# Layer 3 of a four-layer graph kernel: two blocks of sources per step, count rows on four row groups, clamps on two engines

## The chip, the cores and the metric

The kernel runs on one core of a Trainium2 chip. The metric is the device time of one execution in microseconds, from first to last instruction of the core with what lies around it; lower is better. The engines are PE (TensorE: matmuls, with its weight loads listed as PEld), DVE (VectorE), ACT (ScalarE), POOL (GpSimd) and SP (SyncE, which here issues DMAs).

## The reference, cut to what matters

Four graph layers run one after the other on x (4096 x 64) and a 0/1 adjacency adj (4096 x 4096), each on `h = relu(layernorm(x))` and added to x. The change lies in layer 3:

```python
def _L3_gnn_ref(input, adj, weight, bias):          # MAX_NEIGH = 100, DECAY = 0.5
    support = input @ weight
    mask = (adj != 0).astype(support.dtype)
    rank = jnp.cumsum(mask, axis=1)
    deg = rank[:, -1:]
    k = jnp.minimum(deg, float(MAX_NEIGH))
    pos = rank - (deg - k)
    w = mask * jnp.where(pos > 0, DECAY ** (k - pos), 0.0)
    out = w @ support + bias
    return out
```

The last neighbour of a node has weight 1, the one before it 1/2, and so on, so `k - pos` is the number of neighbours that come after this one. Layer 2 just before it needs `adj @ h` and the degrees, then a 128 x 64 product, a relu and a row norm.

The kernel also checks, in every execution, that adj holds only 0 and 1. If it doesn't, a general kernel runs instead; with the given inputs it never does.

## The kernel before, in words

Nodes are in 32 blocks of 128 (`NB = 32`, `P = 128`). adj is given transposed, so sources lie on partitions and targets on the free axis. The mask as one byte per entry lies in DRAM as `mask_d`, in eight groups (`NQ = 8`) of four blocks (`JT = 4`).

The last function, `layers_fast`, holds layers 2 and 3. Layer 2 works in two halves of targets (`hf`). For each half it sums `h` over neighbours, and counts edges per source block and target (`dc`, `cnt16`, 32 rows of counts for each group of 512 targets, four groups on the 128 partitions). Four calls of `layer2_group` follow, each for 512 nodes: a long chain of small steps on PE, DVE and ACT that ends in `SS`, the fp16 high and low parts of `h @ weight`. The last step on DVE of each call is appended to `valued`. Then `plate` multiplies the counts by a triangle, which gives for each source block the number of edges in later blocks, and `late` is that, limited to 128, for half `hf`.

Layer 3 makes four passes `u`, each over 1024 targets (`HO2`, two groups of 512, `NK = 2`). In a pass it goes through the 32 source blocks `j`. For a block it makes the exponent in PSUM, in a tile `pv` of 128 x 1024 fp32 (two banks): first two matmuls with K = 32, which spread the row of `late` for this block to all 128 sources (L2751; the 32 rows are those of the target group, at partitions `r` to `r + 31`); then two matmuls of the triangular matrix `tri` with the mask bytes (L2759), which subtract the edges that follow inside the block. ACT clamps the result at 0 and writes it as int16 (L2768); those bits, read as bf16, are the power of two. Two matmuls with the `SS` of the block add them up in PSUM (`sacc`, L2733), one step late: the sums of block `j - 1` are written behind the exponent of block `j`. After 32 blocks the sums go through `ev`, a small product with `fold_3` and two additions to `out`.

The checks of adj use one half row block each: `count_odd` asks for 128 x 2048 fp32 (1 MB) into `raw` (two buffers, L954) and compares it on DVE (L955). There are 64 checks; 48 are done in layer 1, and 16 are written into layer 3, one at every block with `j % 8 == 4`. `tc.issue_after(valued[-1].ins)` keeps the DVE part of them behind the last step of layer 2 there.

The order on each engine is not the order of the text. The kernel's framework has a planner which goes through all instructions before the run, with estimates of duration, and gives each engine the earliest in the text among those whose inputs and buffers are ready; that order is then fixed, and each engine waits on semaphores in it. The number of buffers of a tile (`bufs`) therefore limits how far a load or a step runs ahead. Only some stretches before layer 3 have an order set by hand (`in_order`). PSUM in layer 3 has eight banks: two of `misc`, two of `sacc`, four of `pv`.

Of the kernel before, what the change touches and what calls it, by code (L numbers as in the profile page):

```python
# [9 lines left out]
F32 = mybir.dt.float32  # L10
BF16 = mybir.dt.bfloat16
F16 = mybir.dt.float16
F8 = mybir.dt.float8e4
I32 = mybir.dt.int32
I8 = mybir.dt.int8
I16 = mybir.dt.int16
U8 = mybir.dt.uint8
AF = mybir.ActivationFunctionType
ALU = mybir.AluOpType
AX = mybir.AxisListType  # L20
PSUM = bass.MemoryType.PSUM
# [3 lines left out]
P = 128  # L25
N = 4096
NB = N // P
D = 64
G = 512
NG = N // G  # L30
GB = G // P
JT = 4
# [803 lines left out]
def kernel(  # L836
# [24 lines left out]
    nc = tc.nc  # L861
    NH, F, O = W_sp.shape[0] + W_int.shape[0], W_sp.shape[1], W_sp.shape[2]
# [85 lines left out]

        return col.unsqueeze(2).to_broadcast([P, col.shape[1], width])

    def count_odd(pool, c):

        raw = pool.tile([P, HW], F32, name="raw", tag="raw", bufs=2)
        nc.sync.dma_start(raw, adjT[c % NB * P : (c % NB + 1) * P, c // NB * HW : (c // NB + 1) * HW])  # L954
        nc.vector.scalar_tensor_tensor(  # L955
            raw, raw, 0.0, raw, ALU.is_gt, ALU.not_equal, accum_out=bad[:, c : c + 1]
        )

    todo = iter(range(2 * NB))
# [81 lines left out]
    with ExitStack() as l0:  # L1041
        lp = l0.enter_context(tc.tile_pool(name="l0", bufs=1))
# [258 lines left out]
        with ExitStack() as pa:  # L1301
            hp = pa.enter_context(tc.tile_pool(name="prep", bufs=1))
            work = pa.enter_context(tc.tile_pool(name="pwork", bufs=2))
# [47 lines left out]
            with in_order():  # L1351
                nc.vector.tensor_reduce(fsum, FT[0:F, :], AX.X, ALU.add)
                for b0 in range(0, NB, 8):
                    pw = (ps, ps2)[b0 // 8 % 2].tile([P, 8, KZ], F32, name="pst", tag="misc")
                    for b in range(8):
# [3 lines left out]
                            rhs=rhz,  # L1359
# [1158 lines left out]
    def layers_fast(es, wide, *sums):  # L2518
# [75 lines left out]
        with not_before_nodes():  # L2594
# [25 lines left out]
            nc.vector.tensor_scalar(w3, w3, Q3[0:D], VAL, ALU.mult, ALU.mult)  # L2620
            fold_3 = lp.tile([P, D], F32, name="fold_3f")
            nc.vector.tensor_scalar(fold_3, fold_h, M3, 2.0**27 / VAL, ALU.mult, ALU.mult)
        late = lp.tile([P, 2, G], BF16, name="late")

        def layer2_group(b0, part, deg):

# [47 lines left out]
        with tc.tile_pool(name="ps_nacc", bufs=6, space=PSUM) as ps_acc:  # L2674
            for hf in range(2):
                accs = [ps_acc.tile([P, G], F32, name="nacc", tag="nacc") for _ in range(NS)]
                dc = ps_acc.tile([P, G], F32, name="dc", tag="nacc")
                for q in range(NQ):
                    m = work.tile([P, JT, HW], U8, name="m2", tag="m2", bufs=3)
                    nc.sync.dma_start(m, mask_d[q][hf])  # L2680
                    m8 = m.bitcast(F8)
                    for t in range(JT):
                        j = q * JT + t
                        for k in range(NS):
                            nc.tensor.matmul(  # L2685
                                accs[k],
                                lhsT=HH[:, j].rearrange("p s d -> p (s d)"),
                                rhs=m8[:, t, k * G : (k + 1) * G],
                                start=(j == 0),
                                stop=(j == NB - 1),  # L2690
                            )
                    for t in range(JT):
                        j = q * JT + t
                        for k in range(NS):
                            nc.tensor.matmul(
                                dc[k * O : (k + 1) * O, :],
                                lhsT=sel[:, j * O : (j + 1) * O],
                                rhs=m8[:, t, k * G : (k + 1) * G],
                                start=(j == 0),
                                stop=(j == NB - 1),  # L2700
                            )
                cf = work.tile([P, G], F32, name="cf", tag="cf")
                nc.vector.tensor_copy(cf, dc)
                nc.gpsimd.tensor_copy(cnt16[:, hf], cf)
                ev = work.tile([P, NS, G], F32, name="ev2", tag="ev2", bufs=1)
                for k in range(NS):
                    (nc.vector.tensor_copy if k % 2 else nc.scalar.copy)(ev[:, k, :], accs[k])
                pd = ps.tile([P, GB, NS], F32, name="pdeg", tag="misc")
                for b in range(GB):
                    nc.tensor.matmul(  # L2710
                        pd[:, b], lhsT=cf[:, b * P : (b + 1) * P], rhs=qsel, start=True, stop=True
                    )
                deg = work.tile([P, NS, GB], F32, name="degf", tag="degf")
                nc.vector.tensor_scalar(
                    deg.rearrange("p q b -> p b q"), pd, 1.0, 1.0, ALU.add, ALU.max
                )
                nc.vector.reciprocal(deg, deg)
                for g in range(NS):
                    layer2_group(hf * HB + g * GB, ev[:, g, :], deg[:, g, :])
                pl = ps.tile([P, G], F32, name="plate", tag="misc")  # L2720
                nc.tensor.matmul(pl, lhsT=lat, rhs=cnt16[:, hf], start=True, stop=True)
                nc.vector.tensor_scalar(late[:, hf], pl, VBITS, None, ALU.min)


        ps_acc = es.enter_context(tc.tile_pool(name="ps_sacc", bufs=2, space=PSUM))
        ps_v = es.enter_context(tc.tile_pool(name="ps_v", bufs=2, space=PSUM))
        for u in range(4):
            hs = slice((u % 2) * HO2, (u % 2 + 1) * HO2)
            accs = [ps_acc.tile([P, G], F32, name="sacc", tag="sacc") for _ in range(NK)]

            def add_up(j, w):
                for k in range(NK):
                    nc.tensor.matmul(  # L2733
                        accs[k],
                        lhsT=SS[:, j].rearrange("p s d -> p (s d)"),
                        rhs=w[:, k * G : (k + 1) * G].bitcast(BF16),
                        start=(j == 0),
                        stop=(j == NB - 1),
                    )

            last = None
            for q in range(NQ):
                m = work.tile([P, JT, HO2], U8, name="m3", tag="m3", bufs=3)
                nc.sync.dma_start(m, mask_d[q][u // 2][:, :, hs])
                for t in range(JT):
                    j = q * JT + t

                    pv = ps_v.tile([P, HO2], F32, name="pv", tag="pv")
                    for k in range(NK):
                        r = ((u % 2) * NK + k) * O  # L2750
                        nc.tensor.matmul(  # L2751
                            pv[:, k * G : (k + 1) * G],
                            lhsT=blk[r : r + O, j, :],
                            rhs=late[r : r + O, u // 2, :],
                            start=True,
                            stop=False,
                        )
                    for k in range(NK):
                        nc.tensor.matmul(  # L2759
                            pv[:, k * G : (k + 1) * G],  # L2760
                            lhsT=tri,
                            rhs=m[:, t, k * G : (k + 1) * G].bitcast(F8),
                            start=False,
                            stop=True,
                        )

                    w = work.tile([P, HO2], I16, name="w3b", tag="w3b", bufs=3)
                    nc.scalar.activation(w, pv, AF.Relu)  # L2768
                    if j % 8 == 4:
                        with tc.issue_after(valued[-1].ins):  # L2770
                            count_odd(work, next(todo))
                    if last is not None:
                        add_up(*last)
                    last = (j, w)
            add_up(*last)
            ev = work.tile([P, NK, G], F32, name="ev3", tag="ev3")
            for k in range(NK):
                (nc.vector.tensor_copy if k % 2 else nc.scalar.copy)(ev[:, k, :], accs[k])
            for k in range(NK):
                b0 = (u * NK + k) * GB  # L2780
                pn = ps.tile([P, GB, D], F32, name="pn3", tag="misc")
                for b in range(GB):
                    nc.tensor.matmul(
                        pn[:, b, :],
                        lhsT=ev[:, k, b * P : (b + 1) * P],
                        rhs=fold_3,
                        start=True,
                        stop=True,
                    )
                og = work.tile([P, GB, D], F32, name="og", tag="og")  # L2790
                nc.vector.tensor_tensor(og, pn, b3t.unsqueeze(1).to_broadcast([P, GB, D]), ALU.add)
                nc.vector.tensor_tensor(og, og, x[:, b0 : b0 + GB, :], ALU.add)
                nc.gpsimd.dma_start(  # L2793
                    out[b0 * P : (b0 + GB) * P, :].rearrange("(b p) f -> p b f", p=P), og
                )
# [92 lines left out]
```

## Time and profile before

The kernel took 2023.15 us, the median of three runs (2019.92, 2023.15, 2024.01).

| | |
|---|---|
| time of the profiled execution | 2021.7 us |
| its span, first to last instruction | 2019.9 us |
| mean granted TensorE clock | 0.941 |
| busy: PE, DVE, ACT | 90%, 76%, 73% of the span |
| layer 3, first and last count matmul | 1808.9 to about 2007 us |
| `ev` of passes u = 0 to 3 on DVE | 1877.7, 1921.8, 1965.6, 2009.8 us |
| DMA in the whole span | 239.05 MB, mean 118 GB/s |

Busy times count the time in which an engine works on at least one instruction. A row of the costliest groups names the source line, the engine, the operation, output and inputs, shapes and count, then busy microseconds and the mean nanoseconds of one, and after the bar the idle time just before these instructions and what ended it. Matmuls overlap in PE's pipeline: a duration of some 385 ns is from entry to exit, while the next may start after 215 ns.

### The profile page before, as it was taken

Reading aid. Unit: us, or ns where it says so; the run is one execution under the profiler, and the core shown is the slowest. Engines: PE = TensorE matmul, PEld = TensorE weight load, DVE = VectorE, ACT = ScalarE, POOL = GpSimd, SP = SyncE. Lnnn points to the kernel's source line nnn. Section 1 sums busy time; section 2 is a strip of 40 time slices with the busy share of each in tenths; the row PEclk is TensorE's granted clock in tenths of the full one; section 3 lists DMA queues with packets and bytes.
Section 4 is the critical chain, followed back from the end, with each engine's and each line's share of the span. In section 5 each row is a group of like instructions: output and inputs, shape, how many; then the busy total and the mean of one; then the engine's idle time right before and its main releaser. Section 6 shows DMA issues by size and latency. Waiting matters only on the chain. (4 is left out here: it accounts for less than half of the span.)

```text
span 2019.9 us, 44190 instructions
## 1 busy us (share of the span) xinstructions
PE 1810.5 (90%) x19340; PEld 818.8 (41%) x19340; DVE 1534.4 (76%) x2239; ACT 1474.5 (73%) x1439; POOL 83.4 (4%) x125
## 2 busy tenths in 40 slices
PE   5889989999999999996699958999999985899998
PEld 3444445444444444444244432333333333454332
DVE  6779988998789879996778768888878788533530
ACT  3768888899789888993789857777777743227676
POOL 2000100100000000001011100000000000000000
PEclk8999999999999999997799968999999997889999
DMA  8945564424311111103355415444344336312752
GB/s 112 183 113 100 101 101 65 154 117 172 111 49 49 49 49 54 54 2 96 111 177 194 157 48 199 142 146 153 123 142 150 114 121 221 125 63 73 280 199 65
DMA packets 117016, 239.05 MB, mean 118 GB/s; under 512 B 11062, under 2 KB 84006, under 8 KB 102054
## 3 DMA queue, kind: packets, MB, share of 16 engines
q1 hardware_dynamic: 101996, 192.95, 28.4%
q0 software_dynamic: 14816, 43.18, 11.9%
q8 instruction: 153, 2.51, 0.5%
q14 instruction: 51, 0.42, 0.1%
HBM read 245.37 MB, written 49.46 MB: 146 GB/s over the span
## 5 line engine op out<-in xcount | busy, mean ns | idle before, releaser
L1205 ACT ACTIVATE st<-srow,nt 128x2048 int8<-128x2048 f32 x352 | 682.8, 1994 | 78.4 <-DVE B L1211 77.5
L1211 DVE TENSOR_TENSOR B<-st,mres 128x1024 int32<-128x1024 int32 x256 | 311.7, 1220 | 68.0 <-PE accC L1541 43.5
L1541 PE MATMUL accB<-B,ybh 128*32 128x512 fp8e4 x3072 | 338.7, 384 | 15.6 <-DVE B L1211 15.6
L1541 PE MATMUL accD<-B,ybh 128*32 128x512 fp8e4 x2048 | 301.3, 387 | 21.9 <-DVE h L1657 21.9
L1541 PEld LDWEIGHTS <-ybh 128*32 128x32 bf16 (+1 forms) x6656 | 197.0, 98 | 237.7 <-issue 75.9
L1541 PE MATMUL accC<-B,ycn 128*32 128x512 fp8e4 x2272 | 267.8, 381 | 1.2 <-issue 1.2
L1541 PE MATMUL accC<-mres,ych 128*32 128x512 fp8e4 x2272 | 267.7, 381 | 0.0
L1541 PE MATMUL accL<-B,ybh 128*32 128x512 fp8e4 x1536 | 220.4, 390 | 4.6 <-DVE h L1661 4.5
L1541 PEld LDWEIGHTS <-ych 128*32 128x32 f16 x4096 | 168.7, 98 | 114.5 <-issue 9.1
L1199 DVE TENSOR_SCALAR st<-srow,nt 128x2048 uint8<-128x2048 f32 x160 | 205.4, 1284 | 2.5
L2336 PE MATMUL accj<-sg,who 128*64 128x512 f32 (+1 forms) x512 | 196.6, 614 | 6.5 <-DVE sg L2329 6.1
L2336 PE MATMUL acci<-sg,who 128*64 128x512 f32 (+1 forms) x512 | 196.7, 614 | 0.0
L955 DVE SCALAR_TENSOR_TENSOR raw<-raw 128x2048 f32<-128x2048 f32 x64 | 146.1, 2285 | 33.0 <-DMA raw<-in_adj_dram 32.8
L2292 ACT ACTIVATE yt<-pu,consts 128x512 f32<-128x512 f32 x144 | 98.6, 686 | 98.0 <-PE pu L2291 97.9
L2281 ACT ACTIVATE sg<-pl,rb 128x512 f32<-128x512 f32 x256 | 160.7, 678 | 8.0 <-PE pl L2276 4.9
L2768 ACT ACTIVATE w3b<-pv 128x1024 int16<-128x1024 f32 x128 | 130.9, 1023 | 42.7 <-PE pv L2759 41.2
L1205 ACT ACTIVATE st<-srowo,nto 128x1024 int8<-128x1024 f32 x128 | 138.1, 1137 | 16.4 <-DVE B L1211 14.0
L1541 PE MATMUL accC<-C,ych 128*32 128x512 fp8e4 x1824 | 146.3, 389 | 1.0 <-DVE C L1219 1.0
L1219 DVE TENSOR_TENSOR C<-B,mres 128x1024 int32<-128x1024 int32 x114 | 139.5, 1225 | 3.6
L1541 PEld LDWEIGHTS <-ycn 128*32 128x32 f16 x2272 | 107.7, 97 | 64.2 <-issue 3.6
L2329 DVE SCALAR_TENSOR_TENSOR sg<-pf,sg 128x512 f32<-128x512 f32 x112 | 72.1, 685 | 38.8 <-PE pf L2326 38.8
L2270 PE MATMUL pl<-nm,noid 128*128 128x512 fp8e4 x256 | 82.3, 393 | 13.8 <-ACT sg L2281 12.9
(497 smaller groups left out, 2676.1 us busy)
## 6 DMA issues: line engine op xcount, KB each, us to landing
raw<-in_adj_dram SPq DMA_DIRECT2D x64, 1024.0 KB, 6.2
mo<-edges SPq DMA_DIRECT2D x32, 512.0 KB, 3.9
noedge<-nmo POOLq DMA_DIRECT2D x32, 512.0 KB, 4.1
nm<-noedge SPq DMA_DIRECT2D x64, 256.0 KB, 3.0
m<-edges SPq DMA_DIRECT2D x16, 1024.0 KB, 4.8
m<-edges SPq DMA_DIRECT2D x32, 512.0 KB, 4.9
srow<-srow_d SPq DMA_DIRECT2D x15, 1024.0 KB, 6.8
mres<-in_adj_dram POOLq DMA_DIRECT2D x8, 1024.0 KB, 36.1
```

Of the source, the lines that this page charges most:

```text
L955: nc.vector.scalar_tensor_tensor(raw, raw, 0.0, raw, ALU.is_gt, ALU.not_equal, accum_out=bad[:, c : c + 1])
L1199: nc.vector.tensor_scalar(st[:, i, :].bitcast(U8), srow, negs[:, i : i + 1], EDGE, ALU.is_gt, ALU.mult)
L1205: nc.scalar.activation(st[:, i, :], srow, AF.Sign, bias=negs[:, i : i + 1], scale=-1.0)
L1211: nc.vector.tensor_tensor(B.bitcast(I32), st.bitcast(I32), edges.bitcast(I32), ALU.bitwise_and)
L1219: nc.vector.tensor_tensor(C.bitcast(I32), B.bitcast(I32), edges.bitcast(I32), ALU.bitwise_xor)
L1541: ins = nc.tensor.matmul(acc[k * O : (k + 1) * O, :], lhsT=values, rhs=moving(k), start=start, stop=stop,)
L2270: nc.tensor.matmul(pl, lhsT=noid, rhs=nm[:, b, :].bitcast(F8), start=True, stop=False)
L2281: nc.scalar.activation(sg[:, b0 + k, :], pl, AF.Sigmoid, bias=rb[:, j : j + 1], scale=1.0)
L2292: nc.scalar.activation(far[gi, gj][:, b, :], pu, AF.Sigmoid, bias=nb_t, scale=2.0 * DIST_K / (DIST_S * DIST_S),)
L2329: nc.vector.scalar_tensor_tensor(v[:, t, :], pf, F_K3, v[:, t, :], ALU.add, ALU.mult)
L2336: nc.tensor.matmul(acc[r : r + n, :], lhsT=XQ[:, src, cols], rhs=w, start=start, stop=stop)
L2768: nc.scalar.activation(w, pv, AF.Relu)
```

## The change

It touches layer 3 and the helper of the checks.

- A step treats two source blocks, `j0` and `j0 + 1`. The exponent is in four PSUM tiles of one bank each (`pvs[i, k]`, block i, target group k; pool `ps_v` with 4 instead of 2 buffers, each half as large).
- The four count matmuls of a step stand together and use the four row groups of PE. For this the second block takes its rows from `late_x`, a copy of `late` with the halves of the partitions exchanged, which DVE writes in two more steps for each half.
- The four mask matmuls follow, then the four sums of the pair of blocks before. `w` is 128 x 2 x 1024 in two buffers (before: 128 x 1024 in three).
- The clamp is done per tile: group 0 on DVE, group 1 on ACT, but all four on ACT in a step with `j0 % 8 == 4`, where a check is written.
- `count_odd` is cut in two, `load_rows` and `check_rows`; in layer 3 the rows of a check are asked for directly behind the check before, the first ones ahead of the passes.

```diff
-    def count_odd(pool, c):
+    def load_rows(pool, c):
 
         raw = pool.tile([P, HW], F32, name="raw", tag="raw", bufs=2)
         nc.sync.dma_start(raw, adjT[c % NB * P : (c % NB + 1) * P, c // NB * HW : (c // NB + 1) * HW])
+        return raw, c
+
+    def count_odd(pool, c):
+        check_rows(*load_rows(pool, c))
+
+    def check_rows(raw, c):
+
         nc.vector.scalar_tensor_tensor(
             raw, raw, 0.0, raw, ALU.is_gt, ALU.not_equal, accum_out=bad[:, c : c + 1]
         )
...
-        late = lp.tile([P, 2, G], BF16, name="late")
+        late, late_x = (lp.tile([P, 2, G], BF16, name=n) for n in ("late", "late_x"))
...
                 nc.vector.tensor_scalar(late[:, hf], pl, VBITS, None, ALU.min)
+                for lo, hi in ((slice(0, D), slice(D, P)), (slice(D, P), slice(0, D))):
+                    nc.vector.tensor_scalar(late_x[lo, hf], pl[hi], VBITS, None, ALU.min)
...
-        ps_v = es.enter_context(tc.tile_pool(name="ps_v", bufs=2, space=PSUM))
+        ps_v = es.enter_context(tc.tile_pool(name="ps_v", bufs=4, space=PSUM))
+        rows = load_rows(work, next(todo))
...
-                for t in range(JT):
-                    j = q * JT + t
-
-                    pv = ps_v.tile([P, HO2], F32, name="pv", tag="pv")
-                    for k in range(NK):
-                        r = ((u % 2) * NK + k) * O
+                for t0 in range(0, JT, 2):
+                    j0 = q * JT + t0
+                    both = [(i, k) for i in range(2) for k in range(NK)]
+                    pvs = {ik: ps_v.tile([P, G], F32, name="pv", tag="pv") for ik in both}
+                    for i, k in both:
+                        r = ((u + i) % 2 * NK + k) * O
                         nc.tensor.matmul(
-                            pv[:, k * G : (k + 1) * G],
-                            lhsT=blk[r : r + O, j, :],
-                            rhs=late[r : r + O, u // 2, :],
+                            pvs[i, k],
+                            lhsT=blk[r : r + O, j0 + i, :],
+                            rhs=(late, late_x)[i][r : r + O, u // 2, :],
                             start=True,
                             stop=False,
                         )
...
-                    w = work.tile([P, HO2], I16, name="w3b", tag="w3b", bufs=3)
-                    nc.scalar.activation(w, pv, AF.Relu)
-                    if j % 8 == 4:
+                    w = work.tile([P, 2, HO2], I16, name="w3b", tag="w3b")
+                    for i, k in both:
+                        wk = w[:, i, k * G : (k + 1) * G]
+                        if k == 0 and j0 % 8 != 4:
+                            nc.vector.tensor_scalar(wk, pvs[i, k], 0.0, None, ALU.max)
+                        else:
+                            nc.scalar.activation(wk, pvs[i, k], AF.Relu)
+                    if j0 % 8 == 4:
                         with tc.issue_after(valued[-1].ins):
-                            count_odd(work, next(todo))
+                            check_rows(*rows)
+                            if (u, j0) != (3, NB - 4):
+                                rows = load_rows(work, next(todo))
                     if last is not None:
                         add_up(*last)
-                    last = (j, w)
+                    last = (j0, w)
```

More of the change, by code (lines that the diff above doesn't have):

```diff
@@ L2729, in layers_fast, with add_up @@
             accs = [ps_acc.tile([P, G], F32, name="sacc", tag="sacc") for _ in range(NK)]
-            def add_up(j, w):
-                for k in range(NK):
[L2733 to L2739, printed above, removed]
+            def add_up(j0, w):
+                for i, j in enumerate(range(j0, j0 + 2)):
+                    for k in range(NK):
+                        nc.tensor.matmul(
+                            accs[k],
+                            lhsT=SS[:, j].rearrange("p s d -> p (s d)"),
+                            rhs=w[:, i, k * G : (k + 1) * G].bitcast(BF16),
+                            start=(j == 0),
+                            stop=(j == NB - 1),
+                        )
             last = None
@@ L2744, in layers_fast @@
                 nc.sync.dma_start(m, mask_d[q][u // 2][:, :, hs])
-                for t in range(JT):
-                    j = q * JT + t
-                    pv = ps_v.tile([P, HO2], F32, name="pv", tag="pv")
-                    for k in range(NK):
-                        r = ((u % 2) * NK + k) * O
+                for t0 in range(0, JT, 2):
[4 more added lines that the diff above has]
+                        r = ((u + i) % 2 * NK + k) * O
                         nc.tensor.matmul(
-                            pv[:, k * G : (k + 1) * G],
-                            lhsT=blk[r : r + O, j, :],
-                            rhs=late[r : r + O, u // 2, :],
+                            pvs[i, k],
+                            lhsT=blk[r : r + O, j0 + i, :],
+                            rhs=(late, late_x)[i][r : r + O, u // 2, :],
                             start=True,
@@ L2757, in layers_fast @@
                         )
-                    for k in range(NK):
+                    for i, k in both:
                         nc.tensor.matmul(
-                            pv[:, k * G : (k + 1) * G],
+                            pvs[i, k],
                             lhsT=tri,
-                            rhs=m[:, t, k * G : (k + 1) * G].bitcast(F8),
+                            rhs=m[:, t0 + i, k * G : (k + 1) * G].bitcast(F8),
                             start=False,
@@ L2765, in layers_fast @@
                         )
-                    w = work.tile([P, HO2], I16, name="w3b", tag="w3b", bufs=3)
-                    nc.scalar.activation(w, pv, AF.Relu)
-                    if j % 8 == 4:
+                    w = work.tile([P, 2, HO2], I16, name="w3b", tag="w3b")
+                    for i, k in both:
+                        wk = w[:, i, k * G : (k + 1) * G]
[4 more added lines that the diff above has]
+                    if j0 % 8 == 4:
                         with tc.issue_after(valued[-1].ins):
-                            count_odd(work, next(todo))
+                            check_rows(*rows)
+                            if (u, j0) != (3, NB - 4):
+                                rows = load_rows(work, next(todo))
                     if last is not None:
                         add_up(*last)
-                    last = (j, w)
+                    last = (j0, w)
             add_up(*last)
```

## The prediction

> **What bounds the kernel now.** I first read the page's engine shares and costliest groups, then the groups by shape from 1800 us on (layer 3 runs in the last 211 us), then the windows, then the timeline of single steps. The change touches nothing before about 1806 us, so only this stretch can move.
>
> The groups by shape, from 1800 us to the end (busy us, mean ns, then idle before and what ended it):
> ```profile
> L2768 ACT ACTIVATE w3b<-pv 128x1024 int16<-128x1024 f32 x128 | 130.9, 1023 | 42.7 <-PE pv L2759 41.2 <-PE sacc L2733 1.1
> L2759 PE MATMUL pv<-m,tri 128*128 128x512 fp8e4 x256 | 78.9, 388 | 0.0
> L2733 PE MATMUL sacc<-w3b,XAf 128*128 128x512 bf16 x256 | 78.4, 387 | 2.6 <-ACT XAf L2671 1.6 <-ACT w3b L2768 0.7
> L2751 PE MATMUL pv<-late,LDf 32*128 32x512 bf16 x256 | 52.6, 389 | 0.5 <-ACT w3b L2768 0.5
> L955 DVE SCALAR_TENSOR_TENSOR raw<-raw 128x2048 f32<-128x2048 f32 x16 | 36.6, 2290 | 29.1 <-DMA raw<-in_adj_dram 29.1
> ```
> PE waits for almost nothing (0.0, 2.6, 0.5 us); ScalarE waits for PE. Layer 3 is bound by PE. The count rows (L2751) are 256 instructions of 389 ns, 99.6 us if one followed another, but busy only 52.6: two already run at once.
>
> One step of one source block, from the timeline:
> ```profile
> 1948.33 0.09 PEld L2751 LDWEIGHTS <-LDf 32*128 32x128 bf16 x2 [0.42 <-issue]
> 1948.34 0.39 PE L2751 MATMUL pv<-late,LDf 32*128 32x512 bf16 x2
> 1948.65 0.11 PEld L2759 LDWEIGHTS <-tri 128*128 128x128 bf16 x2 [0.23 <-issue]
> 1948.66 0.60 PE L2759 MATMUL pv<-m,tri 128*128 128x512 fp8e4 x2
> 1948.88 0.10 PEld L2733 LDWEIGHTS <-XAf 128*128 128x128 f16 x1
> 1949.14 0.59 PE L2733 MATMUL sacc<-w3b,XAf 128*128 128x512 bf16 x2
> 1949.36 1.02 ACT L2768 ACTIVATE w3b<-pv 128x1024 int16<-128x1024 f32 x1 [0.27 <-PE pv L2759]
> 1949.66 0.09 PEld L2751 LDWEIGHTS <-LDf 32*128 32x128 bf16 x2 [0.42 <-issue]
> ```
> Read the start times: count pair to masks 0.32, masks to sums 0.48, sums to the next count pair 0.52. A step takes 1.29 to 1.33 us, mean 1.31. One full matmul takes 0.215 us start to start (half of 0.43), so the count pair costs 0.32, not 0.22.
>
> VectorE, in two windows (PE, PEld, DVE, ACT, POOL busy, clock, DMA share, GB/s):
> ```profile
> 1877.00:1946.00 69.00, 68.91 (x329) 23.48 (x328) 37.27 (x41) 50.69 (x51) 3.07 (x4) 1.00 0.87 310
> 1946.00:2009.00 63.00, 62.19 (x292) 20.27 (x291) 2.41 (x7) 47.98 (x48) 1.89 (x3) 1.00 0.25 81
> ```
> and in its own timeline, at the end of pass u = 1:
> ```profile
> 1919.61 2.29 DVE L955 SCALAR_TENSOR_TENSOR raw<-raw 128x2048 f32<-128x2048 f32 x1 [3.84 <-DMA raw<-in_adj_dram]
> 1921.82 0.08 DVE L955 DVE_READ_ACCUMULATOR raw<-raw 128x1 f32 x1
> 1921.82 0.69 DVE L2778 COPY ev<-sacc 128x512 f32<-128x512 f32 x1
> ```
> All 16 checks are over by 1946 us, although the text gives four of them to each of the four passes: the planner, which orders every engine's instructions ahead of the run, moves a check up to wherever its rows arrive. Two run before 1878; the other 14 follow each other every 4.86 us, which is the loop of two buffers: 7.6 us from request to landing (median of the transfer in this stretch) plus 2.3 for the check, halved. They waited 29.1 us for transfers. This cost nothing, as nobody stood behind them on VectorE.
>
> **What the Trainium skill says.** "TensorE: Matmul & The Clock Gate", Part 3, says matmuls on different row groups overlap, and gives 3.07x for four of K=32. The trace agrees for two; no run yet shows four. "TensorEngine Tiling (Array Packing)", Key Properties, says a change of tiling mode drains the array: the 0.10 us above 0.22 here, and 0.09 on the way back, fit that. The same page, Gotcha 1, says row tiles may not share a PSUM bank at the same time, so each of the four needs its own bank, as the change gives it. The first page's architectural detail says VectorE and ScalarE take instructions in strict order; the copy right behind the check above fits.
>
> **Part by part.** The profiled execution took 2021.7 us (span 2019.9); the median of the runs is 2023.15, 1.45 above it. I sum against 2021.7 and add 1.45.
>
> 1. *Two blocks, four row groups.* A pair of blocks takes 2 x 1.31 = 2.62 now. After: one count group 0.32, four masks 0.86 plus 0.02, four sums 0.86 plus 0.09: 2.15 us, 0.47 less. Passes u = 1 to 3 hold 48 pairs: -22.5. Bounds: by the skill's 3.07 the four take 4 x 0.215 / 3.07 = 0.28, 0.065 above one, so -19.5; and -22.5.
>
> 2. *Does the clamp keep up?* There are four PSUM banks and one pair fills them. From the start of a count group the masks start at 0.32, 0.54, 0.75, 0.97, and a clamp may start 0.42 later (0.38 matmul, 0.04 until ACT starts). VectorE: 128x512 from PSUM takes 0.69 (the `late` row, same operation; pitch 0.61), so its clamps run 0.74 to 1.43 and 1.35 to 2.04. ScalarE: 586 ns (the `ev` copy; 1023 less 512 elements gives 0.60), 0.96 to 1.54 and 1.45 to 2.03. Plus 0.06 from ACT's end to PE's start, as now: 2.10 against 2.15. It just keeps up, with nothing to spare. That hides the split; without this cover, each delay on either engine reaches PE.
>
> 3. *Every fourth pair has four clamps on ScalarE.* At a pitch of 0.49 they end at 2.82, so PE waits 0.74. If PE has masks of free banks to run meanwhile, it pays only a broken count group, about 0.2. Twelve such pairs in u = 1 to 3: 0 to +9, taken 0.35 each, +4.
>
> 4. *The checks now stand among clamps on VectorE.* The 14 moved-up checks of 2.25 us meet this: a free stretch of 3.6 us around a ScalarE-only pair costs nothing; otherwise the gap between a pair's clamps is 0.8 us, the next clamp starts at 4.2 instead of 2.9, and PE gets its bank 1.3 late. Two checks fall into four pairs, with one free stretch. Below nothing there is no reason for; upper 14 x 1.3 = 18, plus waits for rows. I take 0.6 each, +8.4: half hit, a little filled by PE. Asking one check ahead issues the same 16 transfers on SP's queue; the planner already asked two ahead, limited by the two buffers, so I cost it at nothing, hidden by that loop. If it changes the order against the mask loads (4.9 us to landing, three buffers), the bound is one late mask, 2 us.
>
> 5. *Pass u = 0* (1809 to 1877 us) runs beside layer 2's last four groups. A group takes 14.9 us: 8 steps of 1.29 plus 4.6 of its own matmuls, and its chain of about 30 instructions on three engines adds up to some 14. PE saves 16 x 0.47 = 7.5, but the chain stays, its VectorE steps now queue behind clamps and its ScalarE steps behind shorter ones. -7.5 to +4, taken -2.
>
> 6. *`late_x`*: two more reads of `plate`, 0.69 each, twice. PE waited 2.1 us at `pdeg` for the one `late` there was, so the first pair delays it by 1.2 to 1.4; at the second, `lo` stands beside it. 0 to 2.8, taken +2. The extra two sums at the very end: 0.43, +0.5.
>
> Sum: -22.5 + 4 + 8.4 - 2 + 2 + 0.5 = -9.6. 2021.7 - 9.6 = 2012.1, plus 1.45: **2013.6 us**.
>
> **Rivals.**
>
> *A, the checks become the bound (slower).* In VectorE's queue a check that waits for its rows holds two clamps, PE's banks and then PE. For it: 29.1 us of such waits in 13 places, and DMA at 310 GB/s with 0.87 busy. Against it: half the stretch has no checks. At 1.7 us each and the full 0.74 for the ScalarE pairs, no gain in u = 0: -22.5 + 9 + 24 + 2.5 = +13: 2036. It decides from about 1.3 us a check on (with my other terms -18 to balance, 18 / 14).
>
> *B, the four do not run together.* The planner fills PE's order with what is ready; near the pass's end it already put one mask matmul among sums (1920.39 us). If it splits the group in two, a pair is 2 x (0.32 + 0.45) + 0.95 + 0.09 = 2.58, -2 over 48 pairs. With more slack the stalls shrink to about +5, less 1 in u = 0, with 2.5 for the rest: about +4 at worst, near 0 to +4: 2025. Against it: the two of now stay together in nearly every step.
>
> *C, the gain nearly whole.* Checks fall in the free stretches and PE fills the rest: -22.5 - 4 + 2 + 2 + 2 + 0.5 = -20: 2003.
>
> **How the numbers follow.** 0.2% is 4 us, about what a measurement of this kernel tells from no change. My forecast has 0.43, C 0.12, A 0.31, B 0.14. So faster 0.54 (the forecast with its lower side and C, less a sliver), same 0.15, slower 0.31. The range runs from C to A's size, 2002 to 2036, leaving about 0.07 below and 0.13 above. The forecast's own range is 2006 to 2020, since cases of both signs matter.
>
> **What would show it.** Right: pairs every 2.15 us late in u = 2 and 3, where no checks are left; L2751's successor with four starts together and a busy sum near a quarter of count times duration; VectorE's clamp near 690 ns, ScalarE's near 590; checks still bunched before about 1945; PE waits for clamps of 6 to 15 us in all. Wrong: PE waiting over 20 us for VectorE clamps, with DMA behind those (A); count rows in twos (B); pairs in quiet stretches above 2.4, where the clamp would not keep up; or u = 0 longer than 68 us.

## The result and the profile after

The change makes the kernel slower: 2031.35 us against 2022.2 us, medians of six runs each, ratio over the single runs 1.0034 with a 95% interval of 1.0017 to 1.0050 (the two medians themselves are 9.2 us apart). The forecast was 2013.6 us and faster; rival A, the checks in front of the clamps, had the right sign. The measured time lies in the stated range of 2002 to 2036 only because that rival's case had been taken into it. The profiled execution of the changed kernel has a span of 2025.5 us, 5.6 above the one of before, and that difference is what the stages below add up to.

First the groups by shape from 1800 us to the end of the changed kernel, as shown for the kernel before:

```profile
L2784 ACT ACTIVATE w3b<-pv 128x512 int16<-128x512 f32 x160 | 87.0, 596 | 78.7 <-PE pv L2770 40.7 <-issue 24.8 <-PE sacc L2744 7.0
L2770 PE MATMUL pv<-m,tri 128*128 128x512 fp8e4 x256 | 73.9, 396 | 0.0
...
L2782 DVE TENSOR_SCALAR w3b<-pv 128x512 int16<-128x512 f32 x96 | 62.6, 685 | 48.9 <-PE pv L2770 41.1 <-ACT w3b L2784 4.3 <-issue 2.2
L2762 PE MATMUL pv<-late_x,LDf 32*128 32x512 bf16 x128 | 37.5, 393 | 5.8 <-DVE w3b L2782 3.8
L962 DVE SCALAR_TENSOR_TENSOR raw<-raw 128x2048 f32<-128x2048 f32 x16 | 36.4, 2287 | 8.3 <-DMA raw<-in_adj_dram 8.3
L2762 PE MATMUL pv<-late,LDf 32*128 32x512 bf16 x128 | 26.9, 394 | 1.2 <-DVE late L2729 0.8 <-ACT w3b L2784 0.3
```

The clamps take what was predicted, 685 and 596 ns. But PE, which waited 0.5 us at the count rows before, now waits 5.8 us at those of `late_x`, mostly for VectorE's clamps. Both clamp engines wait over 40 us for PE; ScalarE did so before (41.2 us), so this alone shows nothing. The waits that are shown for PE are only a part; where PE has other work in its order, a lost slot shows as a count group broken up. Of the 16 groups of four in a pass, 3, 8 and 10 start within 0.05 us in passes 1, 2 and 3; in the kernel without checks (the first experiment) 10 do in each.

One step in a stretch without checks, late in pass 3, from the timeline:

```profile
1986.16 0.39 PE L2762 MATMUL pv<-late,LDf 32*128 32x512 bf16 x2
1986.17 0.39 PE L2762 MATMUL pv<-late_x,LDf 32*128 32x512 bf16 x2
...
1986.49 1.04 PE L2770 MATMUL pv<-m,tri 128*128 128x512 fp8e4 x4
1986.99 1.29 DVE L2782 TENSOR_SCALAR w3b<-pv 128x512 int16<-128x512 f32 x2 [0.89 <-PE pv L2770]
...
1987.19 1.08 ACT L2784 ACTIVATE w3b<-pv 128x512 int16<-128x512 f32 x2 [1.09 <-PE pv L2770]
1987.36 1.03 PE L2744 MATMUL sacc<-w3b,XAf 128*128 128x512 bf16 x4
1988.32 0.10 PEld L2762 LDWEIGHTS <-LDf 32*128 32x128 bf16 x4 [0.42 <-issue]
```

All four count matmuls start within 0.01 us, masks follow 0.33 us after the first, and the step takes 2.16 us (1986.16 to 1988.32) against a forecast of 2.15. The basic step is right. The step that follows two steps later was priced too low:

```profile
1990.81 1.04 PE L2770 MATMUL pv<-m,tri 128*128 128x512 fp8e4 x4
1991.29 2.06 ACT L2784 ACTIVATE w3b<-pv 128x512 int16<-128x512 f32 x4 [0.86 <-ACT w3b L2784]
...
1992.64 0.39 PE L2762 MATMUL pv<-late,LDf 32*128 32x512 bf16 x2
1992.91 0.86 PE L2762 MATMUL pv<-late_x,LDf 32*128 32x512 bf16 x2
1992.91 0.09 PEld L2762 LDWEIGHTS <-LDf 32*128 32x128 bf16 x1 [0.18 <-issue]
1993.70 0.55 PEld L2770 LDWEIGHTS <-tri 128*128 128x128 bf16 x4 [0.70 <-issue]
```

This is a step with four clamps on ScalarE. Their banks come free one after another, the count matmuls follow one by one, and the masks start 1.06 us after the first count matmul instead of 0.33. PE starts nothing else meanwhile: 0.73 us lost, the upper bound of the forecast.

And this is pass 1 on VectorE:

```profile
1885.82 0.68 DVE L2782 TENSOR_SCALAR w3b<-pv 128x512 int16<-128x512 f32 x1
1889.73 2.29 DVE L962 SCALAR_TENSOR_TENSOR raw<-raw 128x2048 f32<-128x2048 f32 x1 [3.23 <-DMA raw<-in_adj_dram]
...
1891.95 0.69 DVE L2782 TENSOR_SCALAR w3b<-pv 128x512 int16<-128x512 f32 x1
```

From 1886.5 to 1891.95 VectorE clamps nothing: it waits 3.23 us for rows, then checks for 2.2. The windows of the same stretch (PE, PEld, DVE, ACT, POOL busy, clock, DMA share, GB/s) show what PE does meanwhile, and its clock:

```profile
1885.00:1890.00 5.00, 3.82 (x12) 0.93 (x12) 1.77 (x5) 1.61 (x4) 0.76 (x1) 0.85 0.98 314
1890.00:1895.00 5.00, 3.20 (x7) 0.68 (x6) 4.25 (x6) 1.19 (x2) 0.00 (x0) 0.50 0.55 174
1895.00:1900.00 5.00, 5.00 (x18) 1.44 (x17) 3.26 (x5) 1.19 (x2) 0.00 (x0) 0.62 0.95 324
1888.50:1898.70 10.20, 8.40 (x22) 2.16 (x22) 7.60 (x9) 2.39 (x4) 0.00 (x0) 0.50 0.76 253
```

Seven matmuls in 5 us, at half clock. The last line shows how long the half clock lasts: 10.2 us, so up to 5.1 us of PE's time in pass 1 went that way. It sets in 2 us after VectorE's last clamp, while VectorE waits for rows; that this stall is its cause is likely but was not tested.

For all kernels I measured the same distances in one profile each, on VectorE: from the first `late` to the `ev` copy of pass 0, and from one `ev` copy to the next. They leave out what happened in the layers before, and the last column gives the ratio of the whole over 5 to 20 runs of each kernel. One thing they do contain is the clock that PE was granted in that one execution. Its mean over pass 1 is 0.90 in the changed kernel, 0.89 in the one with thirds, 0.92 to 0.93 in the other kernels that run whole checks between the new steps, and 0.99 or 1.00 in the rest. In passes 2 and 3 it is 1.00, with one exception (0.96 in pass 2 of "whole checks unpinned"). So differences of up to some 5 us in pass 1, and of 2 us and more in pass 0, may be clock; passes 2 and 3 are the ones to compare. Times in us.

| kernel | pass 0 | pass 1 | pass 2 | pass 3 | passes 1-3 | ratio to before, 95% |
|---|---|---|---|---|---|---|
| before | 71.4 | 44.2 | 43.7 | 44.2 | 132.1 | |
| changed | 73.5 | 51.2 | 42.8 | 41.2 | 135.1 | 1.0034 (1.0017-1.0050) |
| no checks | 71.7 | 38.2 | 41.2 | 41.2 | 120.6 | 0.9951 (0.9936-0.9966) |
| checks pinned | 73.5 | 44.5 | 41.2 | 41.2 | 126.8 | 0.9971 (0.9961-0.9981) |
| no checks, always both engines | 74.3 | 36.1 | 38.5 | 38.2 | 112.8 | 0.9925 (0.9907-0.9942) |
| checks in thirds, both engines | 72.9 | 40.1 | 38.2 | 38.2 | 116.5 | 0.9910 (0.9894-0.9926) |
| the same, pass ends later | 73.1 | 35.8 | 36.7 | 36.6 | 109.0 | 0.9900 (0.9881-0.9919) |
| no checks, count rows in twos | 85.2 | 41.3 | 43.1 | 43.1 | 127.5 | 1.0042 (1.0028-1.0055) |
| no checks, all clamps on ScalarE | 74.1 | 46.2 | 48.2 | 48.2 | 142.6 | 1.0041 (1.0025-1.0058) |
| rows not asked ahead | 73.4 | 50.2 | 44.2 | 41.2 | 135.6 | 1.0014 (1.0000-1.0027) |
| whole checks unpinned, both engines | 74.6 | 47.9 | 44.6 | 38.2 | 130.7 | 1.0001 (0.9989-1.0013) |
| before, with `late_x` | 75.7 | 43.5 | 44.0 | 44.2 | 131.7 | 1.0033 (1.0013-1.0053) |
| whole checks pinned, both engines | 74.6 | 44.4 | 41.9 | 41.9 | 128.3 | 0.9993 (0.9979-1.0007) |

### The profile page after: what moved, and what is told of

It is laid out like the page before. It is cut to its first block, busy times and chain, and to the rows that moved or that the text cites. A ratio compares the mean times of both kernels' runs of the same rounds, so it can differ in the third digit from the quotient of the medians.

```text
span 2025.5 us, 44269 instructions
## 1 busy us (share of the span) xinstructions
PE 1805.6 (89%) x19323; PEld 824.9 (41%) x19340; DVE 1597.2 (79%) x2339; ACT 1431.3 (71%) x1471; POOL 83.9 (4%) x125
## 3 DMA queue, kind: packets, MB, share of 16 engines
q0 software_dynamic: 14816, 43.18, 11.9%
## 5 line engine op out<-in xcount | busy, mean ns | idle before, releaser
L2784 ACT ACTIVATE w3b<-pv 128x512 int16<-128x512 f32 x160 | 87.0, 596 | 78.7 <-PE pv L2770 40.7
L2782 DVE TENSOR_SCALAR w3b<-pv 128x512 int16<-128x512 f32 x96 | 62.6, 685 | 48.9 <-PE pv L2770 41.1
```

Source lines behind the costliest of these rows:

```text
L2782: nc.vector.tensor_scalar(wk, pvs[i, k], 0.0, None, ALU.max)
L2784: nc.scalar.activation(wk, pvs[i, k], AF.Relu)
```

## The experiments

**No checks.** Edit to the changed kernel: the calls and the transfers in layer 3 are gone.

```diff
-                    if j0 % 8 == 4:
-                        with tc.issue_after(valued[-1].ins):
-                            check_rows(*rows)
...
```

> The changed kernel with the 16 checks of layer 3 and their transfers left out. Theory V (the checks stand in front of clamps in VectorE's queue, about 0.84 us each for 14 of them, and nothing else is wrong with passes 1 and 2): the distance from the ev copy of one pass to the next on VectorE is about 41.2 us in passes 1, 2 and 3 alike (now 51.2, 42.8, 41.2), and the time falls by some 12 us to about 2019. Rival R (the new order on PE, count groups broken in twos and ones, costs the time; the checks are innocent): pass 1 stays near 50 us and the time within 4 us of the changed kernel.

Measured: median 2013.11 us, and pass 2 at 41.16, exactly pass 3. Pass 1 fell from 51.2 to 38.2, more than forecast; why it is shorter than the others here was not looked into. Passes 1 to 3 lose 14.6 us: 12.9 in pass 1, where ten of the checks had run, 1.6 in pass 2 with four, nothing in pass 3 with none. The two lines are pass 1 as one window, in the changed kernel and in this one; the clock (0.90 and 1.00) is part of the difference:

```profile
1880.15:1931.34 51.19, 45.47 (x190) 14.77 (x192) 39.62 (x52) 20.50 (x38) 1.56 (x2) 0.90 0.87 296
1880.25:1918.49 38.24, 37.84 (x203) 14.58 (x199) 16.28 (x27) 20.70 (x40) 1.56 (x2) 1.00 0.33 106
```

Rival R falls: without the checks 10 of pass 1's 16 count groups stay whole instead of 3, so most of the breaking came with the checks and not with the new order.

**Checks pinned to their place.** The checks and their 16 MB are all there; only their place in VectorE's queue is set.

```diff
-                            nc.vector.tensor_scalar(wk, pvs[i, k], 0.0, None, ALU.max)
+                            clamp = nc.vector.tensor_scalar(wk, pvs[i, k], 0.0, None, ALU.max)
...
-                        with tc.issue_after(valued[-1].ins):
+                        with tc.issue_after(valued[-1].ins), tc.issue_after(clamp.ins):
```

> The changed kernel, each check also kept behind the last VectorE clamp written ahead of it, so that it runs in the step whose clamps are all on ScalarE. All transfers and checks are there. Theory V: a check there costs nothing; pass 2 and pass 3 take about 41.2 us, pass 1 about 43 because the four checks of pass 0 still come together at its start; time about 2020 to 2022. Rival D (the transfers of the rows compete with the mask loads or slow the engines, not the place in the queue): the same 16 MB moves, so passes 1 to 3 together keep their extra 11 us and the time stays near 2030. Rival R: no change.

Measured: passes 2 and 3 both 41.16 us, with eight checks in them, the same as with none. Median 2017.31 us: one more order edge turns the slower kernel into one that beats the kernel before. The timeline in pass 3:

```profile
1988.86 2.28 DVE L962 SCALAR_TENSOR_TENSOR raw<-raw 128x2048 f32<-128x2048 f32 x1
...
1989.00 0.39 PE L2762 MATMUL pv<-late,LDf 32*128 32x512 bf16 x2
...
1989.33 1.04 PE L2770 MATMUL pv<-m,tri 128*128 128x512 fp8e4 x4
1989.80 2.06 ACT L2784 ACTIVATE w3b<-pv 128x512 int16<-128x512 f32 x4 [0.86 <-ACT w3b L2784]
```

The check starts with the step whose four clamps are ScalarE's and ends before the next clamp of VectorE is due. That is the place which the text gives it and the planner took away. Rival D falls too: the transfers all took place. Pass 1 keeps 44.5 against 38.2. It holds six checks, since two of pass 0's four still run at its start, and its mean clock is 0.92; how much each of the two costs was not separated.

**No checks, both engines in every step.** One further edit: `if k == 0 and j0 % 8 != 4:` becomes `if k == 0:`.

> As the kernel without the 16 checks of layer 3, and in every step group 0 is clamped on VectorE and group 1 on ScalarE. If the steps with four clamps on ScalarE cost 0.75 us each: every step takes 2.16 us, a pass 38.2 us, about 9 us less than the kernel without checks over three passes and 1 to 3 more in pass 0, about 2008. If PE fills those waits with other work, as the prediction had it by half: 4 us less, about 2014. Rival R: under 2 us.

Measured: pass 3 takes 38.2, 2.95 less than without the edit, or 0.74 for each of its four steps. The full wait is paid there; over passes 1 to 3 the edit saves 7.8 us, 0.65 a step. The whole went from 2013.11 to 2009.38 us only: pass 0 grew by 2.6 us. There VectorE also carries layer 2's chain, but the clock was lower too (0.87 against 0.90 from the first `late` to the second, worth up to 2.2 us); which of the two it was is open.

**Checks in thirds.** Each check in parts of 704, 704 and 640 columns, a part behind the clamps of every step of passes 1 to 3, both engines clamping in all. The rows of two checks are asked for ahead of the passes.

```diff
+                    if u > 0:
+                        third = ((u - 1) * NB + j0) // 2 % 3
+                        cs = (slice(0, 704), slice(704, 1408), slice(1408, HW))[third]
...
+                        with tc.issue_after(valued[-1].ins), tc.issue_after(clamp.ins):
+                            nc.vector.scalar_tensor_tensor(
+                                raw[:, cs], raw[:, cs], 0.0, raw[:, cs], ALU.is_gt, ALU.not_equal,
...
```

> All checks done, but each in three parts of 704, 704 and 640 columns, one part behind the VectorE clamps of each step of passes 1 to 3, and clamps on both engines in every step. A part takes some 0.87 us with its accumulator read; the gap between the clamps of two steps is 0.93 us. Theory V: it just fits, a pass takes 38 to 39 us, the time is 2009 to 2013, below the kernel before. If the parts don't fit the gap, each delays the next clamp by 0.1 to 0.3 us: a pass of 40 to 43 us, 2015 to 2024. Rival D: as in the pinned kernel, near 2030.

Measured: 2006.11 us, below the forecast; passes 2 and 3 take the 38.2 us of the kernel without checks. Pass 1 takes 40.1 instead of 36.1, at a mean clock of 0.89 against 0.99, which is worth up to 4 us. The parts (881 and 815 ns) fit the gap:

```profile
1952.93 0.88 DVE L2791 SCALAR_TENSOR_TENSOR raw<-raw 128x704 f32<-128x704 f32 x1
...
1953.73 0.08 DVE L2791 DVE_READ_ACCUMULATOR raw<-raw 128x1 f32 x1
1953.88 1.29 DVE L2782 TENSOR_SCALAR w3b<-pv 128x512 int16<-128x512 f32 x2
```

**Pass ends later.** In addition the `ev` copies, the product and the output of a pass are written behind the first step of the next one.

```diff
                     if last is not None:
                         add_up(*last)
+                    elif u > 0:
+                        ended()
```

> As the kernel with checks in thirds, and the end of a pass (ev copies, the product with fold_3, output) is written behind the first step of the next pass. Theory: between two passes 3.65 us are lost beyond 16 steps of 2.16 us, 2.0 for the product and the rest because the masks of the next pass stand behind it on PE while both clamp engines idle 3 us; with the masks first, a pass takes 36.5 to 37 instead of 38.2 us and the time falls by 3 to 5 us to about 2002. Rival: the sums' banks come free later, so the wait only moves to the next sums: 38.2 as before.

Measured: 36.6 and 36.7 us a pass, 2003.13 us, the fastest version. The 16 steps alone take 16 x 2.16 = 34.6 us; of the 3.65 us between passes about 2 are left, as much as the product itself takes (2.00). In pass 1, 35.8 against 40.1 us, most of the difference may be clock (0.99 against 0.89).

**Count rows in twos.** From the kernel without checks and with both engines: two count matmuls and two masks of block `j0`, then those of `j0 + 1`.

> As the kernel without checks and with both engines clamping in every step, but the count rows stand in twos: two count matmuls and two masks of the first block, then those of the second. If a count group costs 0.32 us however many run in it, and 0.1 for the way back, a step takes 2.16 + 0.32 + 0.1 = 2.58 us, a pass 43 to 45, the time about 2026: the four row groups are then the whole gain per step. If the clamps have hidden something else, the step is 2.3 or less and the time under 2016.

Measured: steps of 2.58 us as worked out, passes 2 and 3 of 43.1 us, and a pass 0 of 85.2, more than forecast; its mean clock up to the second `late` is 0.80, against 0.87 with the groups of four. Ratio 1.0042. So the gain of a step is the joint count group: 0.42 us, the entry and the way back saved once per step.

```profile
1983.13 0.39 PE L2763 MATMUL pv<-late,LDf 32*128 32x512 bf16 x2
...
1983.45 0.61 PE L2771 MATMUL pv<-m,tri 128*128 128x512 fp8e4 x2
...
1983.99 0.39 PE L2763 MATMUL pv<-late_x,LDf 32*128 32x512 bf16 x2
...
1984.31 0.60 PE L2771 MATMUL pv<-m,tri 128*128 128x512 fp8e4 x2
...
1984.75 1.03 PE L2744 MATMUL sacc<-w3b,XAf 128*128 128x512 bf16 x4
...
1985.71 0.39 PE L2763 MATMUL pv<-late,LDf 32*128 32x512 bf16 x2
```

**All clamps on ScalarE**, no checks.

> The changed kernel without checks, all four clamps of every step on ScalarE. If four of them hold PE for 0.75 us per step as in the steps of every fourth pair, a step takes 2.91 us, a pass 48 to 50, and the time is about 2040. If ScalarE can catch up when it has nothing else, a step takes 2.62 at most (four clamps of 0.60 with pitches of 0.49 are 2.07 us of work) and the time is 2022 or less.

Measured: steps of 2.91 us, passes of 48.2, as the first case had it, in a profile with a span of 2035.0 us. The median of the runs, 2030.68, is lower than the forecast. ScalarE does not catch up: with four banks in use, its last clamp, the next count group and the next masks form one loop.

**Rows not asked ahead.** `check_rows(*rows)` becomes `count_odd(work, next(todo))` in its place, and the loads ahead go.

> The changed kernel with each check's rows asked for at its own place in the text again. Prediction's step 4: the planner asks ahead as far as two buffers allow in either text, so nothing changes: ratio to the kernel before 1.000 to 1.006, pass 1 near 51 us. Rival: asking ahead does shorten the waits for rows on VectorE (8.3 us with it); without it they are nearer 29 us and the time is 2040 or more.

Measured: ratio 1.0014; passes 1 to 3 take 135.6 against 135.1, VectorE waits 11.7 us for rows instead of 8.3. The interval just meets that of the changed kernel's ratio. Asking ahead changes nothing that can be seen.

**Whole checks, unpinned, both engines in every step.** In the changed kernel `if k == 0 and j0 % 8 != 4:` becomes `if k == 0:`; the checks stay as they are.

> The changed kernel with both engines clamping in every step; whole checks, left to the planner. If the steps with four clamps on ScalarE gave the moved-up checks a free place (half of them, by the prediction's step 4), those checks now cost 1.3 us each: passes 1 to 3 take 113 us without checks plus 14 x 1.3, 131 us, against 135 in the changed kernel; time 2022 to 2027. If those steps gave them no place at all, the checks cost what they cost now (14.6 us in passes 1 to 3) and 12 x 0.75 us are saved: 127 to 128 us, 2019 to 2022. If they were what kept it from getting worse: 2035 or more.

Measured: 130.7 us for passes 1 to 3, the first case: 17.9 above the same without checks, 1.28 us for each of 14, with waits for rows and lost clock in it. With the ScalarE-only steps it is 14.6 / 14 = 1.04. The means hide two different passes. In pass 2 four checks cost 6.0 us here and 1.6 with the ScalarE-only steps, so there these steps did give free places. In pass 1 ten checks cost 11.9 us here and 12.9 with them: nothing was caught that can be seen.

**`late_x` alone in the kernel before.**

> The kernel before with the two further reads of plate that write late_x (used by nothing). From the first late on VectorE to the ev copy of pass 0 it takes 71.4 us in the kernel before and 73.5 in the changed one. If late_x is what lengthens pass 0: 72.8 to 73.5 us here. If the clamps in pass 0 do it: 71.4 to 71.8. The time of the whole cannot tell 2 us: ratio 0.999 to 1.002.

Measured: pass 0 takes 75.7 us, 4.3 more, beyond the first case. About a third is plain: from the second `late` to `ev` it takes 6.90 instead of 5.36 us, since the two further reads (1.39) stand ahead of the two checks there; the changed kernel has 6.91. The rest lies in the chain before, 68.8 instead of 66.0 us, where the planner found another order on PE and where the mean clock was 0.90 instead of 0.93, worth up to 2.3 us; the changed kernel has 66.6 at 0.90. Which of the two it was is open. The ratio of the whole, 1.0033, is beyond the forecast too.

**Whole checks pinned, both engines in every step.** The pinned kernel with the same edit.

> As the kernel with pinned checks, and both engines clamp in every step: a whole check of 2.25 us always stands between the clamps of two steps whose gap is 0.9 us. By the prediction's working a check there costs 1.3 us in full: passes 2 and 3 take 38.2 + 4 x 1.3 = 43.4 us. If PE fills the wait with other work, 40 or less; if the delay also breaks the count groups of the steps behind it, 45 or more.

Measured: passes 2 and 3 take 41.9 us, 3.7 above 38.2, or 0.93 per check instead of 1.3. A check inside a pass lengthens a step from 2.16 to 3.20 us, by 1.04; the one at the pass's end costs about 0.5. It lies between the cases: in the step at 1955.85 us PE starts three of the four count rows and one mask before the last held bank comes free.

## Why the prediction was wrong, point by point

The profiled spans differ by +5.6; the prediction's sum was -9.6.

*Step 1, the pair* held: 48 x (2.16 - 2.62) = -22.1, forecast -22.5. The 3.07 of the Trainium skill ("TensorE: Matmul & The Clock Gate", Part 3), taken as the price of a group of four, would have put the masks 0.065 us later than behind a pair; they come 0.33 us after the first count matmul instead of 0.32.

*Step 2, the clamp keeps up* held, with less room than worked out. The durations were right (685 and 596 ns), but a clamp starts 0.10 to 0.11 us after its mask matmul has ended, not 0.04. In the quiet step above VectorE's second clamp ends 2.12 us after the first count matmul, not 2.04, and the next group starts 0.04 us later.

*Step 3, four clamps on ScalarE* was mis-sized: 0.74 each in a quiet pass, the upper end, times twelve is +9 instead of +4 (over the three passes 7.8 was measured). I let PE fill the wait with masks of free banks. PE's order is fixed before the run, and there the four count rows stand ahead of all masks; nothing behind them could start.

*Step 4, the checks* is the step that failed: +14.6 in passes 1 to 3 instead of +8.4, so 1.04 us instead of 0.6 for each of the 14. The "half hit" failed in pass 1. I read from the profile of before that the planner moves checks to wherever rows arrive, and then gave half of them a free place all the same; the free places are known to the text alone. The ten checks that ended up in pass 1 cost 12.9 us, 1.3 each, so that no free half can be seen there; the four in pass 2 cost 0.4 each, less than forecast. The sum also had nothing for two things. The waits for rows, which I had named only beside the upper bound, held VectorE, with clamps behind them in its queue, for 7.4 us in pass 1. And up to 5.1 us of PE's time went by half clock there, which no term had. A check in the way, with neither, cost 1.04 inside a pass and not 1.3, by which ten would be 10.4: an estimate from the last experiment. How the 12.9 us divide among place, rows and clock no run separates. Asking one check ahead was costed at nothing, and was nothing.

*Steps 5 and 6, pass 0*: 0 forecast, +2.2 measured. `late_x` costs 1.5 at its second place, as step 6 allowed. The gain of 2 in step 5 did not come: the chain takes 66.6 instead of 66.0 us, at a mean clock of 0.90 against 0.93, worth up to 2.0 us in this profile. From the first count matmul to the end of the pass it took 72.8 us, beyond the 68 that had been named as a sign of being wrong (before, measured the same way: 68.8).

*Between passes*: before, 132.1 less 96 steps of 1.31 leave 6.3 us; now 120.6 less 48 steps of 2.16 and twelve waits of 0.75 leave 7.9. That is +1.5, a remainder for which the prediction had no term; its +0.5 was for two more sums at the very end. Where the next pass's masks no longer stand behind the product, passes 2 and 3 are 1.5 and 1.6 us shorter.

The sum of what was measured: -22.1 + 9 + 14.6 + 2.2 + 1.5, and 0.3 from before the first `late`, is +5.5, against +5.6 of the spans. It must come out near, as the term between passes is what the others leave.

*Rival A* named the mechanism, waits for rows included, and the break-even of 1.3 us per check with my other terms. With the ScalarE steps at their full 0.74 the balance comes down to about 0.9, and the checks cost 1.04. Its sign, PE waiting over 20 us for VectorE's clamps, did not show: PE's marked waits for clamps are 5.7 us in all, below even the 6 to 15 that were to mean right. The better sign was the busy sum of the count rows, 49.3 of 100.9 us, half instead of a quarter. *Rival B* did not happen in quiet stretches; in pass 1, 13 of 16 groups were broken, against 6 without the checks. *Rival C*'s 2003 us needed checks that all fall into free places. They don't fall there by themselves; cut in thirds and tied to their gaps they do, at 2006 us, and with the later pass ends at 2003.

## What to carry to other kernels

When a step on the critical path is given to an engine that had only side work, that side work moves onto the path with it; what it cost before (29 us of waits, all free) says nothing of what it costs then. If a free place for it was made in the text, check that the scheduler puts it there, or set an order edge: here one edge was worth 8 us of passes 1 to 3. And cut side work to the size of the gap: in passes 2 and 3 three parts of 0.9 us were free where one check of 2.3 us cost 0.9.

## What the runs showed of the hardware that was not expected

- Four K = 32 matmuls on four row groups cost PE no more than two: masks start 0.32 to 0.33 us after the first count matmul in both kernels.
- A read of 64 partitions by 512 columns from PSUM takes VectorE 688 ns (`late_x`), as long as one of 128 partitions (691 and 685 ns).
- PE's granted clock was 0.50 for 10.2 us of pass 1 in the changed kernel. It set in within a stretch of 5.5 us in which VectorE clamped nothing and PE had little to do. In the kernel without checks the windows at the same times have 1.00. These are single profiles, and other kernels with checks also show half clock in pass 1, for other lengths of time.
